# A four-layer graph network on one core: the last layer as seven block products merged by TensorE, gate values kept in PSUM, and a plan that models the shared port

## The chip, the cores and the metric

The kernel runs on one core of one Trainium2 chip. The metric is the device time of one execution in microseconds; the time of the kernel is the median of its runs. The engines are TensorE (PE; its weight loads are PEld), VectorE (DVE), ScalarE (ACT), GpSimd (POOL) and SyncE (SP), which issues nearly all DMA transfers. PSUM, into which TensorE writes, has eight banks of 512 float32 columns; the kernel calls them slots.

## The reference

x is 64 graphs of 256 nodes with 128 features; adj is one 256 x 256 adjacency matrix that all graphs share. Four layers follow each other, each with a residual and a layer norm. Two are attention layers. The third is a gated network of five steps. The fourth is a graph convolution with powers of adj. Cut to what matters:

```python
def _L2_gnn_ref(input, in_matrix, out_matrix, ...):
    def step(h, _):
        m_in = jnp.einsum('nm,bmd->bnd', in_matrix, h)
        m_out = jnp.einsum('nm,bmd->bnd', out_matrix, h)
        av = jnp.concatenate([m_in, m_out], axis=-1)
        u3 = h @ u3_w.T + u3_b
        z = jax.nn.sigmoid(av @ w3_w.T + w3_b + u3)
        r = jax.nn.sigmoid(av @ w4_w.T + w4_b + u3)
        hv = jnp.tanh(av @ w5_w.T + w5_b + (r * h @ u5_w.T + u5_b))
        h = (1.0 - z) * h + z * hv
        return (h, None)
    h, _ = jax.lax.scan(step, input, None, length=5)
    return h

def _L3_gnn_ref(x_1, adj0, adj1, weight_1):
    # _chebyshev(adj, x, 3): adj @ x, adj^2 @ x, adj^3 @ x, stacked
    parts = [x_1[..., None], _chebyshev(adj0, x_1, 3), _chebyshev(adj1, x_1, 3)]
    x_all = jnp.concatenate(parts, axis=3)
    return jnp.einsum('bnik,iok->bno', x_all, weight_1)

x = _layernorm(x + _L0_gnn_ref(x, adj, ...), axis=-1)
x = _layernorm(x + _L1_gnn_ref(x, adj, ...), axis=-1)
x = _layernorm(x + _L2_gnn_ref(x, adj, adj, ..., 5), axis=-1)
x = _layernorm(x + _L3_gnn_ref(x, adj, adj, L3_gnn_weight_1), axis=-1)
```

Since adj0 and adj1 are the same matrix, the last layer is x W0 + A x W1 + A² (x W2 + A x W3) with four combined weights, W0 holding the identity of the residual too.

## The kernel before

The 64 graphs go through in 32 units of two graphs. A unit's tile has 128 partitions and four blocks of 128 columns (two graphs, two halves of the nodes). Ten units are in flight, each in its own lane of SBUF buffers; a lane takes its next unit when it has finished one. All arithmetic is float32.

**The order.** No loop fixes what runs next. `spawn` writes a unit's operations down as tasks, each with its engine, a duration in ns, and what it reads and writes. `Plan.run` then plays a clock: each engine takes, among the tasks whose inputs are there and whose PSUM slots are free, the one with the smallest key, and is busy for the duration given; the result is visible to others after LATENCY. The key (`first`) is the unit's number times PERIOD, plus the task's due time (durations and latencies along its dependences, times PACE or, in the third layer, PACE_GATED), less HASTE for a task on a slot already open. The outcome is one fixed list for each engine, and the chip runs these lists in order with semaphores between them. So a wrong duration in the plan costs nothing by itself, but an instruction that waits on the chip holds all that stands behind it on its engine, of every unit.

**The left product** (`left_fast`, L833 to L878, matmuls all at L844) computes adj times a tile by seven 128-column products in place of eight. GpSimd forms three sums of blocks (`block_sums`, L833, L835, L836), TensorE makes seven products into two slots, ScalarE copies two of them out (L856, L859), VectorE merges (L865, L875, L877, L878). The second product accumulates on the first in its slot after L856 has copied the first out.

**The gated step** (`layer2`) makes five 512-column products (`product`, all at L902): three into slot ps_g (for r, then z added on it) and two into ps_v. ScalarE takes tanh of r (L914), of z (L922) and of the candidate v (L931) into SBUF tiles, which the profile calls e and p. VectorE does four 512-wide operations: (r+1) h (L917), (z-1) h (L929), (z+1) v (L933), and the sum (L935). Then a block transpose (L943 or L956) and DMA transfers through DRAM bring the state into the other layout. ps_g is free again when L922 has read it.

**The last layer** (`layer3`) makes one left product, then, for units 0 to 28, eight 256-column products with the four weights (L1004), two copies by ScalarE (L1009, L1010), block sums by VectorE, seven 128-column products with blocks of the squared adjacency (in `one`, L1015), a copy (L1028) and five merges by VectorE. The last PLAIN = 3 units use `layer3_end`: eight 256-column products with the weights (L1051), two copies (L1055), four 256-column products with the squared adjacency (L1058). A layer norm and the transfer to the output follow.

Of the kernel before, what the change touches and what calls it, by code (L numbers as in the profile page):

```python
# [13 lines left out]
P = 128  # L14
# [18 lines left out]
PERIOD = 46000.0  # L33
TAIL = 0.3
LATE = 6
PACE = 3.0
PACE_GATED = 1.65
# [4 lines left out]
HASTE = {"pe": 10000.0, "act": 10000.0, "dve": 10000.0}  # L42
PLAIN = 3
# [4 lines left out]
class Cell:  # L48


    def __init__(self, ap=None, bank=False, over=()):
        self.ap, self.bank = ap, bank

        self.over = list(over)
        for c in over:
            c.over.append(self)
        self.writers, self.readers, self.users = [], [], 0
        self.group, self.waits = None, set()


class Task:
    def __init__(self, eng, ns, fn, unit, wait, dma):
        self.eng, self.ns, self.fn, self.unit, self.wait, self.dma = eng, ns, fn, unit, wait, dma
        self.step, self.layer = 0, 0
        self.deps, self.then, self.left, self.at = set(), [], 0, 0.0
        self.off = self.end = self.due = 0.0
        self.banks, self.takes = [], []


class Plan:  # L70
# [5 lines left out]
    LATENCY = {"pe": 500, "dve": 400, "act": 400, "pool": 500, "sp": 3500}  # L76
# [4 lines left out]
    def __init__(self, banks):  # L81
        self.free_banks = list(banks)
        self.tasks = []
        self.unit, self.step, self.layer = -1, 0, 0

        self.rank = None

    def add(self, eng, ns, fn, reads=(), writes=(), after=(), wait=0, group=None, dma=False):
        t = Task(eng, ns, fn, self.unit, wait, dma or eng == "sp")
# [27 lines left out]

    def run(self, spawn, units, key):
# [4 lines left out]
        free = dict.fromkeys(ready, 0.0)  # L123
        seen, now, running = 0, 0.0, []
# [16 lines left out]
        def start(lane):  # L141
            mine = [u for u in queue if u % LANES == lane]
            if mine:
# [5 lines left out]
                for t in self.tasks[seen:]:  # L149
                    t.due = max([d.due + (PACE_GATED if t.layer == 2 else PACE) * (d.ns + (  # L150
                        d.wait + self.LATENCY["sp" if d.dma else d.eng] if d.dma or d.eng != t.eng else self.OWN[t.eng]))
                        for d in t.deps if d.unit == t.unit], default=0.0)
                enlist()
# [4 lines left out]
        while any(ready.values()) or running:  # L158

            for t in [t for t in running if t.end <= now]:  # L160
                running.remove(t)
                for c in t.banks:
                    c.users -= 1
                    if not c.users:
                        self.free_banks.append(c.ap)
# [3 lines left out]
            for e, tasks in ready.items():  # L169
# [3 lines left out]
                fit = [t for t in tasks if t.at <= now + (HOLD if now < START else 0) and len(t.takes) <= len(self.free_banks)]  # L173
                if not fit:
                    continue
                t = min(fit, key=key)
# [3 lines left out]
                for c in t.takes:  # L180
                    c.ap = self.free_banks.pop(0)
                order.append(t)
                free[e] = t.off = now + t.ns
# [20 lines left out]
def kernel(  # L204
# [51 lines left out]
    def bank():  # L256
        return Cell(bank=True)
# [5 lines left out]
    def lane_cells(k):  # L263
# [8 lines left out]
        for at, halves in (("e", (("r", "ex"), ("z",))), ("p", (("v",), ("xT1",)))):  # L272
            for half, names in enumerate(halves):
                over = [c[at]]
                for name in names:
                    c[name] = Cell(c[at].ap.rearrange("p g n -> p (g n)")[:, half * T : (half + 1) * T], over=over)
                    over = [*over, c[name]]
        c["x"] = cell(f"x_{k}", [P, UB, NC, D])
# [213 lines left out]
    w3 = cell("w3", [D, 2, 2, D])  # L492
    add(POOL, 480, lambda: nc.gpsimd.tensor_add(w3.ap[:, 0, 1, :], wk.ap[:, :, 0], ident.ap), (wk, ident), (w3,))
    for k in range(1, 4):
        add(POOL, 480, lambda k=k: nc.gpsimd.tensor_add(
            w3.ap[:, k % 2, 1 - k // 2, :], wk.ap[:, :, k], wk.ap[:, :, k + 3]), (wk,), (w3,))
# [10 lines left out]
    fast_blocks(a2f, a2T)  # L507
    plan.rank = None


    X = {}

# [7 lines left out]
    def small(u, what, ns, op, reads, writes, **more):  # L520

        pool = u >= TIGHT and what in SMALL
        add(POOL if pool else DVE, 300 if pool else ns, lambda: op(nc.gpsimd if pool else nc.vector), reads, writes, **more)
# [56 lines left out]
    def layernorm(u, L, pairs, swap=False, centred=False):  # L580
# [11 lines left out]
        add(POOL, 1150, lambda: nc.gpsimd.tensor_tensor(rstd.ap, ve.ap, nhalf.ap, op=ALU.pow), (ve, nhalf), (rstd,))  # L592
        by_act = u >= TIGHT and plan.layer in NORM

        if by_act and not centred:
            mean = st.ap.rearrange("p k (j s) -> p k j s", j=2)[:, :, :, 1]
            if "shift" in SMALL:
                add(POOL, 330, lambda: nc.gpsimd.tensor_scalar_mul(
                    nm.ap.rearrange("p (k j) -> p k j", k=2), mean, -1.0), (st,), (nm,))
                add(POOL, 250, lambda: nc.gpsimd.tensor_mul(ve.ap, nm.ap, rstd.ap), (nm, rstd), (ve,))  # L600
# [48 lines left out]
    def layer0(u, L):  # L649
# [47 lines left out]
        for b in range(UB):  # L697
            add(DVE, 540, lambda b=b: nc.vector.tensor_add(
                ev[:, b, :, 0:P].rearrange("p k (c i) -> p k c i", c=NC), rv()[:, b].rearrange("p c (i k) -> p k c i", k=2),
                neg0.ap[:, :, 0:P].rearrange("p k (c i) -> p k c i", c=NC)), (row, neg0), (e,), group=es)  # L700
# [23 lines left out]
        if not SCALES or u < TIGHT:  # L724
            add(DVE, 700, lambda: nc.vector.tensor_mul(
                h.ap[:, :, 0 : D + 2], h.ap[:, :, 0 : D + 2],
                rs.ap.rearrange("p (g o) -> p g o", o=1).to_broadcast([P, G, D + 2])), (h, rs), (h,))
# [28 lines left out]
    def layer1(u, L):  # L756
# [6 lines left out]
        for bs in [[b] for b in range(UB)] if u < HALVES else [list(range(UB))]:  # L763
# [3 lines left out]
            for b in bs:  # L767
# [7 lines left out]
                mask1.ap.rearrange("p (o c) n -> p o (c n)", o=1).to_broadcast([P, n, NC * N])), (ec, mask1), (pc,))  # L775
# [36 lines left out]
        add(DVE, 600, lambda: nc.vector.scalar_tensor_tensor(hp.ap, ex.ap, 1.0, hp.ap, op0=ALU.min, op1=ALU.max), (ex, hp), (hp,))  # L812
        add(DVE, 630, lambda: nc.vector.tensor_add(hp.ap, hp.ap, xf), (hp, X[u]), (hp,))
# [11 lines left out]
    def block_sums(src, blk, s, by_pool):  # L825
# [5 lines left out]
        wide, narrow = (780, 580) if by_pool else (350, 215)  # L831

        add(by, wide, lambda: eng.tensor_sub(  # L833
            four[:, 0:2], blk(slice(2, 3)).to_broadcast([P, 2, D]), blk(slice(0, 4, 3))), (src,), (s,), group=ss)
        add(by, narrow, lambda: eng.tensor_sub(four[:, 2:3], four[:, 1:2], blk(slice(0, 1))), (src, s), (s,), group=ss)  # L835
        add(by, narrow, lambda: eng.tensor_add(four[:, 3:4], four[:, 2:3], blk(slice(1, 2))), (src, s), (s,), group=ss)  # L836
        return four

    def left_fast(src, blk, mat, s, p1, m, by_pool):
# [26 lines left out]
        merged(y, m, ms)  # L866

# [12 lines left out]
    def layer2(u, L):  # L880
        h, ht = turned(u, L, -1), X[u]
        for step in range(STEPS):
# [3 lines left out]
            if fast and not step:  # L886
                left_fast(ht, lambda g, ht=ht: ht.ap.rearrange("p b c d -> p (b c) d")[:, g], adjf, L["r"], L["z"], m, step in BY_POOL)
            elif fast:
                left_fast(ht, lambda g, ht=ht: gd(ht.ap)[:, g], adjTf, L["r"], L["z"], m, step in BY_POOL)
# [9 lines left out]
            ps_g, ps_v = bank(), bank()  # L899

            def product(ps, w, c, rhs, start, stop, after=()):
# [5 lines left out]
            merge = plan.tasks[at:][-4:]  # L907
            product(ps_g, lambda: gT.ap[:, 3], gT, h, True, False, merge[2:3] if fast else lefts[1:2])
# [5 lines left out]
            add(ACT, 590, lambda ps_g=ps_g, up=up: nc.scalar.activation(  # L914
                r.ap, ps_g.ap, AF.Tanh, bias=bias2.ap[:, 1:2], scale=0.5 / up), (ps_g, bias2), (r,))
            tanh_r = list(r.writers)
            add(DVE, 650, lambda h=h: nc.vector.scalar_tensor_tensor(r.ap, r.ap, 1.0, h.ap, op0=ALU.add, op1=ALU.mult),  # L917
                (r, h), (r,))
            product(ps_v, lambda: gT.ap[:, 2], gT, m, True, False, tanh_r)
            product(ps_g, lambda: gT.ap[:, 0], gT, m, False, True)  # L920
            product(ps_v, lambda: u5T.ap[:, 0], u5T, r, False, True)
            add(ACT, 590, lambda ps_g=ps_g, up=up: nc.scalar.activation(  # L922
                z.ap, ps_g.ap, AF.Tanh, bias=bias2.ap[:, 0:1], scale=0.5 / up), (ps_g, bias2), (z,))

            new = L["xT1" if h is L["xT0"] else "xT0"]
            if not step:
                add(ACT, 600, lambda h=h, new=new, part=part: nc.scalar.mul(new.ap, h.ap, part), (h,), (new,))
                h = new
            add(DVE, 650, lambda h=h, new=new: nc.vector.scalar_tensor_tensor(  # L929
                new.ap, z.ap, -1.0, h.ap, op0=ALU.add, op1=ALU.mult), (z, h), (new,))  # L930
            add(ACT, 590, lambda ps_v=ps_v, up=up: nc.scalar.activation(  # L931
                v.ap, ps_v.ap, AF.Tanh, bias=bias2.ap[:, 2:3], scale=1 / up), (ps_v, bias2), (v,))
            add(DVE, 650, lambda: nc.vector.scalar_tensor_tensor(v.ap, z.ap, 1.0, v.ap, op0=ALU.add, op1=ALU.mult),  # L933
                (v, z), (v,))
            add(DVE, 650, lambda new=new, part=part: nc.vector.scalar_tensor_tensor(  # L935
                new.ap, v.ap, part, new.ap, op0=ALU.mult, op1=ALU.subtract), (v, new), (new,))
# [36 lines left out]
        if far(u, STEPS - 1):  # L973
            add(DVE, 600, lambda: nc.vector.tensor_add(
                y.ap.rearrange("p (g a i) -> p g a i", g=G, i=BL), ht.ap.rearrange("p (a g i) -> p g a i", g=G, i=BL),
                X[u].ap.rearrange("p b c (a i) -> p (b c) a i", i=BL)), (ht, X[u]), (y,))
# [6 lines left out]
    def layer3(u, L):  # L983
        xT = turned(u, L, STEPS)
        aT, s = L["m"], L["z"]
        if STEPS in FAST and far(u, STEPS):
            left_fast(X[u], lambda g: X[u].ap.rearrange("p b c d -> p (b c) d")[:, g], adjf, L["r"], L["z"], aT, STEPS in BY_POOL)
            tail = [t for t in plan.tasks[-4:-3]]
# [11 lines left out]
        x, y = bank(), bank()  # L1000
        home = {(0, 0): (x, slice(0, 2)), (1, 1): (x, slice(2, 4)), (0, 1): (y, slice(0, 3, 2)), (1, 0): (y, slice(1, 4, 2))}
        for k, src in enumerate((xT, aT)):
            for (b, c), (ps, at) in home.items():
                add(PE, mm_ns(N), lambda k=k, src=src, c=c, b=b, ps=ps, at=at: nc.tensor.matmul(  # L1004
                    gd(ps.ap)[:, at], bn(src.ap)[:, b, c * P : (c + 1) * P], w3.ap[:, k],
                    start=(k == 0 and b == 0), stop=(k == 1), skip_group_check=True), (src, w3), (ps,), tail)
        four, sv = gd(L["xT1"].ap), gd(s.ap)
        copies = object()
        add(ACT, 270, lambda: nc.scalar.copy(sv[:, 0:4:3], gd(x.ap)[:, 0:3:2]), (x,), (s,), group=copies)  # L1009
        add(ACT, 270, lambda: nc.scalar.copy(sv[:, 1:3], gd(y.ap)[:, 0:2]), (y,), (s,), group=copies)  # L1010
        block_sums(s, lambda g: sv[:, g], L["xT1"], -1 in BY_POOL)
        t, p1, out = L["xT1"], L["v"], L["ht"]

        def one(ps, at, lhs, c, k, start, after=()):
            return add(PE, mm_ns(P) + 4, lambda: nc.tensor.matmul(  # L1015
                ps.ap[:, at * P : (at + 1) * P], a2f.ap[:, k // NC, k % NC * P : (k % NC + 1) * P], lhs(), start=start,
                stop=True, skip_group_check=True), (c, a2f), (ps,), after, group=four)

        def d(g):
            return lambda: sv[:, g]  # L1020

        def sm(k):
# [95 lines left out]
```

The softmax here doesn't subtract the row's maximum and nothing guards it: scores larger than these inputs give would overflow.

## Time and profile before

| | before |
|---|---|
| median of 3 runs | 1388.74 us (1388.68 to 1389.56) |
| the profiled run: time, span of the profile | 1389.4 us, 1387.4 us |
| instructions in the profile | 23,294 |
| granted TensorE clock | 1.00 |
| HBM traffic | 81.10 MB read, 64.46 MB written, 105 GB/s |

The span runs from the first to the last instruction of the profile. Busy times are those of one execution; a float32 product of the program stands in the trace as two matmul records. An operation is named by its line, its engine and its tiles (written <- read), where `ps` is any of the eight slots. The chain of waits follows the work that ended last back to the start. Idle time of an engine that does not bound the kernel costs nothing.

### The profile page before, as it was taken

The numbers are of one execution on the slowest core, as the hardware profiler recorded it, in microseconds if no ns is written. First come the engines' busy times: TensorE is split into PE (matmuls) and PEld (weight loads), VectorE is DVE, ScalarE is ACT, GpSimd is POOL, SyncE is SP. The second block draws the span as 40 slices with busy tenths as digits, with TensorE's granted clock in tenths as the row PEclk, the third lists the DMA queues.
The fourth block names the chain that finished last, engine by engine and source line by source line (L and its number), as shares of the span: only waits on it lengthen the run. The fifth ranks groups of instructions, "written<-read, shape, count | busy, mean of one in ns | idle before, by whom it ended". The sixth has DMA issues, their size and how long they took to land.

```text
span 1387.4 us, 23294 instructions
## 1 busy us (share of the span) xinstructions
PE 1379.3 (99%) x6891; PEld 966.9 (70%) x6891; DVE 1195.8 (86%) x2745; ACT 943.7 (68%) x2303; POOL 629.9 (45%) x1039
## 2 busy tenths in 40 slices
PE   9999999999999999999999999999999999999998
PEld 9776666766676766676766777777666666667777
DVE  6978999998888898888988798899888888998865
ACT  5887656666766777766677678887766655565544
POOL 4234343534355454455354454465443533536433
PEclk9999999999999999999999999999999999999999
DMA  4224545454555555554545554545454454554322
GB/s 129 38 47 103 113 106 106 109 128 111 113 121 107 108 123 105 120 115 104 119 109 115 116 119 115 110 110 121 107 128 100 104 108 95 112 124 115 82 65 61
DMA packets 530077, 147.13 MB, mean 106 GB/s; under 512 B 456480, under 2 KB 495136, under 8 KB 529952
## 3 DMA queue, kind: packets, MB, share of 16 engines
q1 hardware_dynamic: 529152, 145.13, 47.0%
q8 instruction: 55, 0.90, 0.3%
q14 instruction: 70, 0.57, 0.2%
q10 hardware_dynamic: 800, 0.52, 0.1%
HBM read 81.10 MB, written 64.46 MB: 105 GB/s over the span
## 4 chain that ended last, share of the span: by engine, by line
PE 91%; DVE 6%; ACT 1%; issue 1%; POOL 1%; DMA 0%; SPq 0%; POOLq 0%; DVEq 0%; ACTq 0%
PE ps L902 45%; PE ps L844 19%; PE ps L1004 7%; PE ps L743 4%; PE ps L780 4%; PE ps L1015 3%; PE ps L738 2%; PE ps L667 2%; PE ps L792 2%; PE ps L821 1%; PE ps L1051 1%; DVE p L933 1%; DVE st L587 1%; DVE p L546 0%; DVE e L917 0%
## 5 line engine op out<-in xcount | busy, mean ns | idle before, releaser
L902 PE MATMUL ps<-m,gT 128*128 128x512 f32 x960 | 478.6, 593 | 0.0
L902 PEld LDWEIGHTS ps<-m,gT 128*128 128x128 f32 x960 | 166.1, 191 | 113.0 <-issue 91.5
L833 POOL TENSOR_TENSOR e<-ht 128x256 f32<-128x256 f32 x121 | 104.3, 862 | 210.1 <-DMA ht<-hb 153.5
L844 PEld LDWEIGHTS ps<-adjTp,ht 128*128 128x128 f32 x726 | 124.0, 191 | 82.7 <-issue 73.3
L914 ACT ACTIVATE e<-ps,bias 128x512 f32<-128x512 f32 x160 | 109.9, 687 | 95.0 <-PE ps L902 88.4
L931 ACT ACTIVATE p<-ps,bias 128x512 f32<-128x512 f32 x160 | 109.7, 686 | 85.2 <-PE ps L902 83.9
L902 PE MATMUL ps<-e,u5T 128*128 128x512 f32 x320 | 163.2, 593 | 0.0
L592 POOL TENSOR_TENSOR rstd<-ve,nhalf 128x4 f32<-128x4 f32 x126 | 143.6, 1141 | 34.8 <-DVE ve L589 29.8
L589 POOL TENSOR_SCALAR ve<-st 128x4 f32<-128x4 f32 x110 | 38.4, 349 | 259.3 <-DVE st L587 231.3
L844 PE MATMUL ps<-adjTp,e 128*128 128x128 f32 x968 | 149.6, 275 | 0.0
L922 ACT ACTIVATE e<-ps,bias 128x512 f32<-128x512 f32 x160 | 109.8, 688 | 55.5 <-PE ps L902 55.2
L844 PEld LDWEIGHTS ps<-adjTp,e 128*128 128x128 f32 x968 | 130.5, 192 | 13.8 <-issue 11.1
L844 PE MATMUL ps<-adjTp,ht 128*128 128x128 f32 x726 | 138.9, 275 | 0.3 <-DMA ht<-hb 0.2
L933 DVE SCALAR_TENSOR_TENSOR p<-e,p 128x512 f32<-128x512 f32 x160 | 115.2, 721 | 19.4 <-ACT p L931 19.1
L902 PEld LDWEIGHTS ps<-e,u5T 128*128 128x128 f32 x320 | 58.9, 190 | 63.8 <-issue 49.0
L611 ACT ACTIVATE x<-ht,ve,rstd 128x128 f32<-128x128 f32 x212 | 92.4, 489 | 14.3 <-POOL ve L600 14.2
L902 PE MATMUL ps<-xT,gT 128*128 128x512 f32 x192 | 98.0, 593 | 0.0
L875 DVE TENSOR_TENSOR m<-ps,m 128x256 f32<-128x256 f32 x182 | 75.0, 412 | 18.5 <-PE ps L844 17.3
L833 POOL TENSOR_TENSOR e<-x 128x256 f32<-128x256 f32 x61 | 48.7, 798 | 91.8 <-ACT x L611 78.5
L769 ACT ACTIVATE e<-m,esd 128x256 f32<-128x256 f32 x116 | 84.3, 767 | 0.5 <-DMA m<-row 0.5
L917 DVE SCALAR_TENSOR_TENSOR e<-e,xT 128x512 f32<-128x512 f32 x96 | 68.6, 715 | 16.4 <-ACT e L914 15.6
L844 PEld LDWEIGHTS ps<-adjT,x 128*128 128x128 f32 x366 | 60.7, 191 | 29.2 <-issue 24.8
(211 smaller groups left out, 3201.9 us busy)
## 6 DMA issues: line engine op xcount, KB each, us to landing
hb<-p SPq DMA_DIRECT2D x182, 256.0 KB, 2.3
ht<-hb SPq DMA_DIRECT2D x484, 64.0 KB, 2.5
xT<-hb SPq DMA_DIRECT2D x244, 64.0 KB, 2.5
m<-row SPq DMA_DIRECT2D x58, 256.0 KB, 3.7
hb<-p SPq DMA_DIRECT2D x124, 64.0 KB, 1.8
ht<-hb SPq DMA_DIRECT2D x31, 256.0 KB, 2.8
out_dram<-x SPq DMA_DIRECT2D x30, 256.0 KB, 2.5
m<-in_x_dram SPq DMA_DIRECT2D x88, 64.0 KB, 2.4
```

The costliest lines, as they stand in the source:

```text
L592: add(POOL, 1150, lambda: nc.gpsimd.tensor_tensor(rstd.ap, ve.ap, nhalf.ap, op=ALU.pow), (ve, nhalf), (rstd,))
L611: add(ACT, 400, lambda j=j, b=b, ch=ch, view=view, at=at, shift=shift, col=col: nc.scalar.activation(X[u].ap[:, b, ch, :], view()[:, j, :] ...
L769: add(ACT, 660 if u >= DIRECT_ROWS else 360, lambda g=g, b=b: nc.scalar.activation(e.ap[:, g, :].rearrange("p (c n) -> p c n", c=NC), ev() ...
L833: add(by, wide, lambda: eng.tensor_sub(four[:, 0:2], blk(slice(2, 3)).to_broadcast([P, 2, D]), blk(slice(0, 4, 3))), (src,), (s,), group=ss)
L844: add(PE, mm_ns(P) + 4, lambda: nc.tensor.matmul(ps.ap[:, at * P : (at + 1) * P], lhs(), mat.ap[:, k, c * P : (c + 1) * P], start=start, s ...
L875: add(DVE, 335, lambda: nc.vector.tensor_tensor(mv[:, 1:3], pv(y)[:, 0:2], mv[:, 3:4].to_broadcast([P, 2, P]), op=ALU.add), (y, m), (m,))
L902: add(PE, mm_ns(T), lambda: nc.tensor.matmul(ps.ap, w(), rhs.ap, start=start, stop=stop, skip_group_check=True), (c, rhs), (ps,), after)
L914: add(ACT, 590, lambda ps_g=ps_g, up=up: nc.scalar.activation(r.ap, ps_g.ap, AF.Tanh, bias=bias2.ap[:, 1:2], scale=0.5 / up), (ps_g, bias2 ...
L922: add(ACT, 590, lambda ps_g=ps_g, up=up: nc.scalar.activation(z.ap, ps_g.ap, AF.Tanh, bias=bias2.ap[:, 0:1], scale=0.5 / up), (ps_g, bias2 ...
L931: add(ACT, 590, lambda ps_v=ps_v, up=up: nc.scalar.activation(v.ap, ps_v.ap, AF.Tanh, bias=bias2.ap[:, 2:3], scale=1 / up), (ps_v, bias2), ...
L933: add(DVE, 650, lambda: nc.vector.scalar_tensor_tensor(v.ap, z.ap, 1.0, v.ap, op0=ALU.add, op1=ALU.mult), (v, z), (v,))
L1004: add(PE, mm_ns(N), lambda k=k, src=src, c=c, b=b, ps=ps, at=at: nc.tensor.matmul(gd(ps.ap)[:, at], bn(src.ap)[:, b, c * P : (c + 1) * P], ...
```

## The change

1. **The last layer of units 0 to 27** goes from `layer3` to a new `layer3_blocks`. The weight is treated as the squared adjacency was: a 2 x 2 block matrix, in seven products in place of eight. Each of the seven multiplies two 128-row halves, so it is a pair of 128-column matmuls; the four sums of inputs are made by GpSimd on 256 columns. Merging moves to TensorE: ScalarE copies a product that several results share from slot x to slot y ("seeds" it), and later products accumulate on that seed or on what lies in x already. A seeded slot has to be one all of whose columns a matmul has written before, which `Cell.full`, `seeded_bank`, `fits` and `take` keep track of.
2. **PLAIN** goes from 3 to 4: unit 28 takes the form of the last units. The two halves of w3 change places, and `fast_blocks(w3f, w3)` makes four more weight blocks in the setup.
3. **Gates**: tanh of z is written back to ps_g, and VectorE writes z times v there; tanh of r and of v stay in SBUF. The z product of m is listed ahead of the first v product.
4. **The plan**: VectorE operations with two SBUF inputs and all GpSimd operations are marked `port`. A marked one starts after the other engine's marked one has let go, and after a marked VectorE task another one gets TURN = 12000 added to its key. Several durations and latencies change. HASTE applies to a task between two uses of a slot (`hold`, `within`), and VectorE gets none. PERIOD, LATE, PACE and PACE_GATED change.

```diff
-PERIOD = 46000.0
+PERIOD = 41000.0
-LATE = 6
-PACE = 3.0
-PACE_GATED = 1.65
+LATE = 5
+PACE = 4.0
+PACE_GATED = 1.56
-HASTE = {"pe": 10000.0, "act": 10000.0, "dve": 10000.0}
-PLAIN = 3
+HASTE = {"pe": 45000.0, "act": 45000.0}
+IN_PSUM = (0, 1, 0, 1)
+TURN = 12000.0
+PLAIN = 4
...
-    LATENCY = {"pe": 500, "dve": 400, "act": 400, "pool": 500, "sp": 3500}
+    LATENCY = {"pe": 400, "dve": 350, "act": 350, "pool": 900, "sp": 4000}
...
-                t = min(fit, key=key)
+                t = min(fit, key=lambda t: key(t) + (TURN if twice and t.port and e == "dve" else 0))
...
-                free[e] = t.off = now + t.ns
+                begin = now
+                if t.port:
+                    begin = max(now, held["pool" if e == "dve" else "dve"])
+                free[e] = t.off = begin + t.ns
...
-            ps_g, ps_v = bank(), bank()
+            ps_g, ps_v = bank(True), bank(True)
...
+            product(ps_g, lambda: gT.ap[:, 0], gT, m, False, True)
             product(ps_v, lambda: gT.ap[:, 2], gT, m, True, False, tanh_r)
-            product(ps_g, lambda: gT.ap[:, 0], gT, m, False, True)
...
+            tz, tv = ps_g if IN_PSUM[1] else z, ps_v if IN_PSUM[2] else v
+            add(ACT, 590, lambda ps_g=ps_g, up=up, tz=tz: nc.scalar.activation(
+                tz.ap, ps_g.ap, AF.Tanh, bias=bias2.ap[:, 0:1], scale=0.5 / up), (ps_g, bias2), (tz,))
...
+            vv = (v, ps_g, ps_v)[IN_PSUM[3]]
+            add(DVE, 600, lambda tz=tz, tv=tv, vv=vv: nc.vector.scalar_tensor_tensor(
+                vv.ap, tz.ap, 1.0, tv.ap, op0=ALU.add, op1=ALU.mult), (tv, tz), (vv,), port=not (IN_PSUM[1] or IN_PSUM[2]))
+            add(DVE, 600, lambda new=new, part=part, vv=vv: nc.vector.scalar_tensor_tensor(
+                new.ap, vv.ap, part, new.ap, op0=ALU.mult, op1=ALU.subtract), (vv, new), (new,), port=not IN_PSUM[3])
...
+        layer3_blocks(u, L, xT, aT, tail)
...
+        x, y = bank(), seeded_bank()
+        pair(x, 0, x0, xT, 0, tail, True, (y,))
+        first = copied(lambda y=y: part(y, 0, 2), x, 0, 2, y, group)
+        pair(x, 0, sums[2], sb_, 5, [*first, *late])
+        second = copied(lambda y=y: part(y, 2, 2), x, 0, 2, y, group)
+        pair(x, 2, sums[1], sa, 4)
+        copied(lambda: gd2(p1.ap), x, 2, 2, p1, None)
+        pair(y, 0, a0, aT, 2, first)
+        copied(lambda: D4[:, 0:2], y, 0, 2, direct, ds)
+        pair(x, 0, sums[0], sa, 6, second)
+        held = added(gd2(up.ap), 2, x, 0, gd2(p1.ap), (p1,), up, None)
+        pair(y, 2, sums[3], sb_, 3, second)
+        added(E[:, 0:2], 2, y, 2, gd2(p1.ap), (p1,), mv, es)
+        pair(x, 0, a1, aT, 7, held)
+        copied(lambda: D4[:, 2:4], x, 0, 2, direct, ds)
...
+        x, y, os_ = bank(), seeded_bank(), object()
+        square(x, 0, 0, mv, E[:, 0], (), True, (y,))
+        first = copied(lambda: part(y, 0), x, 0, 1, y, group)
+        square(x, 0, 5, four, f[:, 2], first)
+        second = copied(lambda: part(y, 1), x, 0, 1, y, group)
+        square(x, 1, 4, four, f[:, 1])
...
+        square(y, 0, 2, mv, E[:, 1], first)
...
+        square(x, 0, 6, four, f[:, 0], second)
...
+        square(y, 1, 3, four, f[:, 3], second)
...
+        square(x, 0, 7, up, E[:, 5], held)
```

`pair` is two 128-column matmuls, `square` one, `copied` a copy by ScalarE, `added` an addition by VectorE.

## The prediction

> **What bounds the kernel now.** I read four views in this order: busy times, the slices, the chain of waits, and the timeline of TensorE's matmuls. The first three, from the page:
>
> ```profile
> PE 1379.3 (99%) x6891; PEld 966.9 (70%) x6891; DVE 1195.8 (86%) x2745; ACT 943.7 (68%) x2303; POOL 629.9 (45%) x1039
> ...
> PE   9999999999999999999999999999999999999998
> ...
> DVE  6978999998888898888988798899888888998865
> ...
> PEclk9999999999999999999999999999999999999999
> ...
> PE 91%; DVE 6%; ACT 1%; issue 1%; POOL 1%; DMA 0%; SPq 0%; POOLq 0%; DVEq 0%; ACTq 0%
> ```
>
> TensorE is busy in every slice at full clock, and 91% of the chain that ends last is matmuls. But a matmul's end is modelled, so "busy 99%" may hide gaps. What does not lie is the distance between starts, which the timeline of TensorE gives:
>
> ```profile
> 701.15 1.02 PE L902 MATMUL ps<-m,gT 128*128 128x512 f32 x2
> 702.01 0.38 PE L844 MATMUL ps<-adjTp,ht 128*128 128x128 f32 x2
> 702.23 0.39 PE L844 MATMUL ps<-adjT,x 128*128 128x128 f32 x2
> ...
> 706.56 0.83 PE L844 MATMUL ps<-adjTp,e 128*128 128x128 f32 x6
> 707.23 0.39 PE L844 MATMUL ps<-adjT,x 128*128 128x128 f32 x2
> ```
>
> A program's product is two records. A 512-column product takes 702.01 - 701.15 = 0.86 us, a 128-column one 0.22 us: (707.23 - 706.56) / 6 = 0.112 us a record. Over all 6891 records the median distance is 429 ns for 512 columns (1600 records), 216 ns for 256 (900), 112 ns for 128 (3081). Summing what each distance has over its width's median leaves 13.0 us: 4.2 in the first 40 us, 5.8 behind the last matmul, and only 3.0 in the 1340 us between. So TensorE is not merely busy but streaming almost without a gap. A product taken away is worth its distance, and other engines matter only through gaps they cause.
>
> How the last stage reads, from the timeline of the end:
>
> ```profile
> 1356.22 1.06 PE L1015 MATMUL ps<-p,a2T 128*128 128x128 f32 x8
> 1356.42 0.27 ACT L1028 COPY p<-ps 128x128 f32<-128x128 f32 x1
> 1356.47 0.69 DVE L933 SCALAR_TENSOR_TENSOR p<-e,p 128x512 f32<-128x512 f32 x1
> ...
> 1359.92 0.69 DVE L978 TENSOR_TENSOR m<-ps,x 128x512 f32<-128x512 f32 x1
> ...
> 1369.75 1.89 PE L1051 MATMUL ps<-w,xT 128*128 128x256 f32 x8
> ...
> 1371.48 1.89 PE L1051 MATMUL ps<-w,m 128*128 128x256 f32 x8
> ...
> 1379.68 2.19 PE L1058 MATMUL ps<-e,a2T 128*128 128x256 f32 x8
> ```
>
> (1371.48 - 1369.75) / 8 = 0.216 us again. A 512-wide VectorE operation with one input in PSUM (L978) takes 0.69 us, as one with both in SBUF does (L933).
>
> **What the Trainium skill says.** "TensorE: Matmul & The Clock Gate", section on the 56 ns gap: warm matmuls start N / 2.4 GHz plus some 2.5 ns apart, 55.6 ns at N = 128 and 215.7 at 512. The trace agrees at twice these (112 and 429): a float32 record streams its columns twice. So a narrow product pays its fixed cost more often: 2 x 112 = 224 against 216 ns. "SBUF — State Buffer", section Who interferes with whom: a VectorE instruction with two SBUF inputs and a GpSimd one that reads SBUF exclude each other for a whole instruction; with one SBUF input VectorE does not contend. The trace agrees: L875, which reads PSUM, has median 0.414 and 95th percentile 0.425 us; L933, with two SBUF inputs, 0.68 and 1.01; GpSimd's L836 0.46 and 0.94. "PSUM — Partial Sum Buffer", The four PSUM rules: writes by ScalarE or VectorE do not change the bits that decide whether a matmul adds or overwrites, which is what the seeded slots rely on; no row of before shows such a seed.
>
> **The change, part by part.**
>
> *The last layer's products (28 of 32 units).* Before, units 0 to 28 ran 8 products of 256 columns (L1004, 464 records = 29 x 16) and 7 of 128 (L1015, 406 = 29 x 14): 16 x 216 + 14 x 112 = 5024 ns a unit. Units 29 to 31 ran the plain form, 12 products of 256 (24 records): 5184 ns. After, units 0 to 27 run seven pairs for the weight and seven single products for the squared adjacency, 21 of 128 columns: 42 x 112 = 4704 ns; units 28 to 31 run plain. Before: 29 x 5.024 + 3 x 5.184 = 161.2 us. After: 28 x 4.704 + 4 x 5.184 = 152.4 us. **-8.8 us of TensorE**, all on the path.
>
> *Its merges.* VectorE lost three block sums (455, 384, 319 ns) and five merges (413, 413, 283, 414, 278): 2.96 us a unit; it gets three 256-wide adds and four 128-wide ones, 3 x 413 + 4 x 280 = 2.36. In all 29 x 2.96 - 28 x 2.36 = 20 us off. ScalarE goes from two copies of 256 (371) and one of 128 (265), 1.0 us, to five and two, 2.39: 28 x 2.39 - 29 x 1.0 = +38 us, busy 944 to about 982. GpSimd gains five 256-wide (about 0.84) and two 128-wide (0.6) instructions, 5.4 us a unit, 151 us: 630 to 781, 57% of the span. None is the bound, so I price them at nothing: the matmuls of the nine other units in flight lie over them. What they can cost is a TensorE wait: a product on top of a seed waits for the copy that wrote it, some 0.37 us plus the 0.16 us of a matmul's drain (275 - 112 ns), and behind it stand the whole queue's matmuls of all units. Seven such steps a unit. If the order leaves others between, 0; if half of each shows, 7 x 0.27 x 28 = 53 us. The nearest row for how well the order hides this is the left product: its second product waits in the same way for the copy L856, 182 times, and TensorE's gaps of the whole middle are 3.0 us, under 0.02 us each. I take 0; by that row 28 x 7 x 0.02 = 4 us is the upper end.
>
> *z's tanh and z times v in PSUM.* Three of the four VectorE gate operations lose one SBUF input: L929, L933, L935, 160 each, 115.1 + 115.2 + 116.8 = 347 us busy. At 0.685 without contention 480 of them take 329: 18 us off VectorE, which comes to about 1158 us, 84%. ScalarE's and VectorE's writes to PSUM have no row. The PSUM page's table of engine access calls ScalarE faster to PSUM than to SBUF; I allow 0.1 us of their 0.69 either way, 16 us of ScalarE's time in all and as much of VectorE's, off the path while both stay under 90%. The cost is in slots: z's slot was free when tanh z ended and is now held until L935 ends. Over the 160 steps those ends lie 6.03 us apart on average, beside the 6.18 us from the slot's first matmul to the end of tanh z. 160 x 6.03 = 965 us of slot time, of 8 x 1387 = 11,099: 9% more. My sum of what is held now (gate slots 160 x (6.2 + 6.6), left products 182 x (3.6 + 8.0), last layer 29 x 2 x 14, layers 0 and 1 an estimate: seven slots a unit at 5 us, between the 3.6 and 8.0 of the left product) is about 6100, 55%; then some 65%. I take 0 for it; bound below.
>
> *Order and costs in the plan.* The plan's durations, latencies, priorities and the port change the order of one static queue for each engine, not the work. Its latency is 400 ns behind a matmul and 350 behind VectorE and ScalarE. The timeline has a tanh starting 1.06 us after its 512-column product starts, where the plan now allows 1.26; and VectorE 0.72 us after a tanh starts, where it allows 0.94. So it still errs to the safe side. The most it can win is the 3.0 us of middle gaps and a part of the 4.2 and 5.8 at the ends, which I bound at 2 us; it can lose through them as much.
>
> *Free edits.* Five more GpSimd instructions in the setup (blocks of the weight), hidden: the first last layer starts at 168.6 us, and GpSimd is busy 11 of the 40 us from 20 to 60. The swapped halves of w3, the tile names over old buffers and the slot choice move nothing on the chip. SP's queue issues the same transfers in all 32 units; none is moved past another by design.
>
> Sum: -8.8 + 0 + 0 + 0. The span of the profile, 1387.4, comes to 1378.6; the runs lie 1.3 us over it (median 1388.74; the profiled run itself 1389.4), so **1379.9 us**.
>
> **Rivals.** (a) *More than the products*: middle gaps and part of the ends go too, -8.8 - 3 to -5: about 1375.5. For it: less contention, longer latencies allowed behind GpSimd (900 ns) and DMA (4000). Against: only 3 us are there. (b) *Eaten*: the seven dependent steps of the last layer show as waits of some 0.3 us a unit for the seed (28 x 0.3 = 8.4): about 1388, no change. For it: seven round trips TensorE to ScalarE instead of one. Against: 182 left products do that already without a gap. (c) *Slots run out, slower*: with z's slot held twice as long, all eight are at times held by units that wait for VectorE; TensorE then has nothing to open. It decides from 8.8 / 160 = 0.055 us a step on; at 0.12 us a step, 19 us, the time is 1399. For it: the hold doubles in the layer that takes most of the span, and VectorE, which frees the slot, is the second busiest engine. Against: about a third of the slots is free on average, and VectorE's load falls. The change doing something else than it says I see no room for: the products can be counted.
>
> **How the numbers follow.** Forecast 0.60 (1377.5 to 1385, holding the 4 us bound), (a) 0.20, (b) 0.10, (c) 0.10. A difference of 0.2%, 2.8 us, is about what measurement can tell from none: faster is the forecast and (a), 0.80; within, (b), 0.10; slower, (c), 0.10. The range runs from 1374.5 (all middle gaps and 2 us at the ends gone) to 1387: outside are (c), most of (b) and a little below.
>
> **What would show it.** 28 x 28 = 784 records of the weight's pairs and 392 of the square, 7221 records in all, with 112 ns between starts; gaps in the middle of about 3 us again; VectorE near 1158, ScalarE near 982, GpSimd below 781; L929, L933 and L935's successors near 0.685 us with little spread. Wrong if the sum of gaps grows by over 6 us: at seed copies it is (b), at first matmuls of a gate slot (c).

## The result, and the profile after

The changed kernel takes 1382.05 us, median of 4 runs (1382.03 to 1382.75), where the kernel before takes 1389.15 (1388.68 to 1389.72) beside it. The ratio is 0.995, with a 95% interval of 0.9933 to 0.9967: 7.1 us faster, where 8.8 were forecast and 1379.9 us in all. On another chip (run 5) the ratio was 0.9948 (0.9933 to 0.9963).

The busy times, slices and chain of the page after:

```profile
PE 1371.9 (99%) x7221; PEld 970.5 (70%) x7221; DVE 1167.7 (85%) x2709; ACT 972.2 (70%) x2414; POOL 691.3 (50%) x1240
...
PE   9999999999999999999999999999999999999998
...
PEclk9999999999999999999999999999999999999999
...
PE 98%; DVE 1%; ACT 0%; issue 0%; POOL 0%; POOLq 0%; DVEq 0%; ACTq 0%
```

TensorE bounds the kernel as before, now with 98% of the chain. There are 330 records more (7221), although less is streamed: narrow products are counted as often as wide ones. The timeline of TensorE alone shows their pace:

```profile
701.75 0.61 PE L1088 MATMUL ps<-w,xT 128*128 128x128 f32 x4
702.20 0.61 PE L1088 MATMUL ps<-w,p 128*128 128x128 f32 x4
702.65 0.39 PE L904 MATMUL ps<-adjT,x 128*128 128x128 f32 x2
...
704.23 0.46 PE L904 MATMUL ps<-adjTp,e 128*128 128x128 f32 x2
704.52 0.39 PE L904 MATMUL ps<-adjT,e 128*128 128x128 f32 x2
```

L1088 is now every product of the last layer's block form, L904 the left products, L963 the gate products. (702.20 - 701.75) / 4 = 0.112 us a record, the pace of any 128-column product. Between 704.23 and 704.52 lie 0.29 us for two records that need 0.22: a gap of some 70 ns, and such gaps are what the rest of this text counts.

The account is the prediction's: each record at its width's distance (429, 216, 112 ns) is the streamed time; what the distances have over it is gap, up to 40 us, in the middle, and behind the last matmul. From the two traces, in us:

| | span | streamed | before the first | gaps to 40 us | gaps in the middle | behind the last |
|---|---|---|---|---|---|---|
| before | 1387.43 | 1373.06 | 1.35 | 4.23 | 3.07 | 5.73 |
| after | 1380.23 | 1364.26 | 1.34 | 3.03 | 5.86 | 5.75 |
| difference | -7.20 | **-8.80** | 0 | -1.20 | **+2.79** | 0 |

The stream fell by exactly the 8.8 us forecast; 1.6 us of it went back into gaps. (The time is 2.1 us above the forecast; the other 0.5 us is the distance of the time from the span, 1.8 us in the run profiled here where 1.3 were assumed.) On the face of it the case is closed. The runs show that it isn't: the two halves of the change are worth much more, with opposite signs, than the sum tells.

### The profile page after: what moved, and what is told of

It is laid out like the page before. It is cut to its first block, busy times and chain, and to the rows that moved or that the text cites. A ratio compares the mean times of both kernels' runs of the same rounds, so it can differ in the third digit from the quotient of the medians.

```text
span 1380.2 us, 24466 instructions
## 1 busy us (share of the span) xinstructions
PE 1371.9 (99%) x7221; PEld 970.5 (70%) x7221; DVE 1167.7 (85%) x2709; ACT 972.2 (70%) x2414; POOL 691.3 (50%) x1240
## 4 chain that ended last, share of the span: by engine, by line
PE 98%; DVE 1%; ACT 0%; issue 0%; POOL 0%; POOLq 0%; DVEq 0%; ACTq 0%
PE ps L963 50%; PE ps L904 20%; PE ps L1088 10%; PE ps L840 4%; PE ps L803 4%; PE ps L727 2%; PE ps L852 2%; PE ps L798 2%; PE ps L881 1%; PE ps L1157 1%; PE ps L1164 0%; PE ps L405 0%; PE ps L593 0%; PE ps L1031 0%; PE ps L636 0%; PE ps L752 0%
## 5 line engine op out<-in xcount | busy, mean ns | idle before, releaser
L963 PE MATMUL ps<-m,gT 128*128 128x512 f32 x960 | 473.3, 593 | 0.0
L963 PEld LDWEIGHTS ps<-m,gT 128*128 128x128 f32 x960 | 168.0, 191 | 131.8 <-issue 114.4
L975 ACT ACTIVATE e<-ps,bias 128x512 f32<-128x512 f32 x160 | 109.8, 687 | 94.7 <-PE ps L963 85.8
L649 POOL TENSOR_SCALAR ve<-st 128x4 f32<-128x4 f32 x110 | 26.8, 244 | 278.4 <-DVE st L647 269.6
L963 PE MATMUL ps<-e,u5T 128*128 128x512 f32 x320 | 163.5, 592 | 0.0
L904 PEld LDWEIGHTS ps<-adjTp,ht 128*128 128x128 f32 x726 | 118.6, 191 | 61.2 <-issue 48.6
L652 POOL TENSOR_TENSOR rstd<-ve,nhalf 128x4 f32<-128x4 f32 x126 | 137.5, 1091 | 47.5 <-DVE ve L649 41.4
L904 PE MATMUL ps<-adjTp,e 128*128 128x128 f32 x968 | 149.0, 276 | 0.2 <-ACT m L919 0.2
L984 ACT ACTIVATE ps<-ps,bias 128x512 f32<-128x512 f32 x160 | 105.6, 661 | 55.1 <-PE ps L963 54.3
L893 POOL TENSOR_TENSOR e<-ht 128x256 f32<-128x256 f32 x121 | 96.9, 801 | 88.1 <-DMA ht<-hb 73.1
L904 PEld LDWEIGHTS ps<-adjTp,e 128*128 128x128 f32 x968 | 129.6, 192 | 11.9 <-issue 7.9
L996 DVE SCALAR_TENSOR_TENSOR ps<-ps,p 128x512 f32<-128x512 f32 x160 | 110.2, 689 | 32.0 <-ACT p L993 31.4
L904 PE MATMUL ps<-adjTp,ht 128*128 128x128 f32 x726 | 136.7, 275 | 0.0
L963 PEld LDWEIGHTS ps<-e,u5T 128*128 128x128 f32 x320 | 58.7, 190 | 63.1 <-issue 55.5
L963 PE MATMUL ps<-xT,gT 128*128 128x512 f32 x192 | 98.2, 593 | 0.0
L978 DVE SCALAR_TENSOR_TENSOR e<-e,xT 128x512 f32<-128x512 f32 x96 | 72.2, 752 | 12.9 <-ACT e L975 12.4
L919 ACT COPY m<-ps 128x128 f32<-128x128 f32 x182 | 48.0, 268 | 44.0 <-PE ps L904 35.0
```

What stands on the lines that cost most here:

```text
L652: add(POOL, 1010, lambda: nc.gpsimd.tensor_tensor(rstd.ap, ve.ap, nhalf.ap, op=ALU.pow), (ve, nhalf), (rstd,))
L893: add(by, wide, lambda: eng.tensor_sub(four[:, 0:2], blk(slice(2, 3)).to_broadcast([P, 2, D]), blk(slice(0, 4, 3))), (src,), (s,), group=s ...
L904: add(PE, mm_ns(P) + 4, lambda: nc.tensor.matmul(ps.ap[:, at * P : (at + 1) * P], lhs(), mat.ap[:, k, c * P : (c + 1) * P], start=start, s ...
L963: add(PE, mm_ns(T), lambda: nc.tensor.matmul(ps.ap, w(), rhs.ap, start=start, stop=stop, skip_group_check=True), (c, rhs), (ps,), after)
L975: add(ACT, 590, lambda ps_g=ps_g, up=up, tr=tr: nc.scalar.activation(tr.ap, ps_g.ap, AF.Tanh, bias=bias2.ap[:, 1:2], scale=0.5 / up), (ps_ ...
L984: add(ACT, 590, lambda ps_g=ps_g, up=up, tz=tz: nc.scalar.activation(tz.ap, ps_g.ap, AF.Tanh, bias=bias2.ap[:, 0:1], scale=0.5 / up), (ps_ ...
```

## Experiments

Each run stands beside the kernel before on the same chip. Three chips served, and those medians are 1391.09 us on the first (runs 1 to 4), 1390.23 on the second (runs 5 to 8) and 1389.87 on the third (runs 9 to 12). Ratios carry 95% intervals. Gaps are from the trace of one execution of each run. What two traces of the same kernel differ by is seen in run 5: 6.6 us in the middle against 5.9.

**1. The last layer of before in the changed kernel.**

```diff
-PLAIN = 4
+PLAIN = 3
-        layer3_blocks(u, L, xT, aT, tail)
+        x, y = bank(), bank()
+        ...   (the form of before, its weight layout, its layer3_end)
```

> The changed kernel with the last layer, the weight layout and PLAIN = 3 of before put back; gates in PSUM, port model and all constants of the plan stay. Theory A (the time is TensorE's stream plus gaps; the gain is the products): the streamed time is that of before again, 1373.1 us, so 1388 to 1391 us, the whole gain lost. Theory B (the gain comes from the port model and the gates in PSUM, the last layer's saving being eaten by its round trips): 1381 to 1384 us.

Measured: 1388.07 us, ratio 0.9977 (0.9967 to 0.9986). Streamed 1373.06, gaps 2.79 to 40 us, 2.74 in the middle. The stream is back, and the time lies within theory A's range. Not all of the gain goes with it: gates and plan alone are worth 0.2%. In this run GpSimd is busy 551.2 us where it was 629.9 before, so gates and plan take contention away here too, and the gaps in the middle hardly show it (2.7 against 3.1).

**2. The new last layer alone on the kernel before.**

```diff
-IN_PSUM = (0, 1, 0, 1)
+IN_PSUM = (0, 0, 0, 0)
-        t.port = port or eng == "pool"
+        t.port = False
...   (PERIOD, LATE, PACE, PACE_GATED, HASTE, LATENCY, the durations and the order of the z and v products as before)
```

> The kernel before with the new last layer and PLAIN = 4 alone: gates in SBUF, no port in the plan, durations, latencies, priorities and constants of before. Theory A: streamed 1364.3 us, so 1379 to 1384 us, the gain whole or nearly. Theory B: 1387 us or more, since the round trips of the last layer show without the better plan.

Measured: 1400.55 us, ratio 1.0068 (1.0056 to 1.008): slower than before by 9.5 us. The streamed time is 1364.26, as theory A said, but the gaps in the middle are 22.4 us (6.4 of them behind 1355 us, where the work runs out; before has 0.3 there). Theory A fails, and my prediction's "0" for the last layer's merges with it; theory B's range holds.

**3. The changed kernel with its gates in SBUF.**

```diff
-IN_PSUM = (0, 1, 0, 1)
+IN_PSUM = (0, 0, 0, 0)
```

> The changed kernel with tanh of z and z times v in SBUF again (and so marked as users of the port in the plan). Streamed time unchanged, 1364.3 us. Theory A: 1380 to 1384 us, only the gaps may differ by 2 us either way. Theory B: the contention is back, 1385 us or more. Theory C (the longer hold of z's slot made the 2.8 us of added gaps in the middle): 1379 to 1380 us.

Measured: 1397.97 us, ratio 1.005 (1.0036 to 1.0063). Gaps in the middle 22.1 us, about as many as in run 2 without the new plan (22.4, though 6.4 of those lie at the end and only 0.5 here). So the new plan alone does not mend the new last layer. Whether the two tiles in PSUM do, or the order that changed with them, run 9 tells. Theory B's range holds. Theory C, that the longer hold of z's slot made the added gaps, is out. The busy times of this run against those of after show where to look:

```profile
PE 1378.7 (99%) x7221; PEld 970.7 (70%) x7221; DVE 1203.8 (86%) x2709; ACT 974.1 (70%) x2414; POOL 782.6 (56%) x1240
```

The same 1240 GpSimd instructions take 782.6 us instead of 691.3. One place in its timeline (start, duration, engine and line) holds the longest gap:

```profile
253.47 1.21 DVE L833 TENSOR_TENSOR p<-e,mask 128x1024 f32<-128x1024 f32 x1
253.48 2.98 POOL L1080 TENSOR_TENSOR p<-xT,m 128x256 f32<-128x256 f32 x1
...
254.60 0.68 DVE L991 SCALAR_TENSOR_TENSOR xT<-e,p 128x512 f32<-128x512 f32 x1
...
255.20 0.68 DVE L996 SCALAR_TENSOR_TENSOR p<-e,p 128x512 f32<-128x512 f32 x1
...
255.92 1.10 DVE L998 SCALAR_TENSOR_TENSOR xT<-p,xT 128x512 f32<-128x512 f32 x1
...
256.52 0.49 PE L1088 MATMUL ps<-w,p 128*128 128x128 f32 x2 [2.73 <-POOL p L1080]
```

L1080 is one of the four sums of inputs; undisturbed it takes 0.73 us, here 2.98. It was issued at 253.48, 10 ns behind L833; its end at 256.46 less 0.73 is 255.73, some 0.15 us from the end of L996 at 255.88. So it looks as if three VectorE operations, each with two SBUF inputs, went ahead of it, and then L998 took 1.10 us instead of 0.68, as if it had waited in its turn. The profile doesn't show the port itself; this is read from the overlap in time. TensorE stood for 2.73 us. That agrees with what the Trainium skill says in "SBUF — State Buffer", Who interferes with whom: the pair of ports that VectorE and GpSimd share is held for a whole instruction and the other side blocks.

**4. Less to stream, nothing else.** Two of the eight 256-column products of the last layer are left out of the kernel before.

```diff
             for (b, c), (ps, at) in home.items():
+                if k and b == c:
+                    continue
                 add(PE, mm_ns(N), ...
```

> The kernel before without two of the eight 256-column products of the last layer in units 0 to 28 (two of the four that add the adjacency's half; the output leaves these terms out), nothing else changed. Theory A: 29 x 4 records x 216 ns = 25.1 us less, so 1364 us, to within 3 us. Theory B (another engine stands right behind TensorE, VectorE with 86%): at most half of that, 1376 us or more.

Measured: 1368.11 us, ratio 0.9835 (0.9821 to 0.9848), 23 us under before. Streamed 1348.00, that is 25.06 less; gaps in the middle 6.8. Stream turns into time almost one for one, and no other engine becomes the bound within these 25 us. This confirms the bound and refutes theory B of that run.

**5. The changed kernel again**, unchanged, on the second chip.

> The changed kernel as it is, beside the others of this call. All theories: 7 us under the kernel before of the same chip.

Measured: 1382.77 us, ratio 0.9948 (0.9933 to 0.9963); gaps in the middle 6.6.

**6. Is it the new sums on GpSimd?** Run 3 with the four L1080 left out of each unit; the tasks stay in the plan, so that every engine keeps its order.

```diff
-            add(POOL, 705, lambda k=k, i=i, op=op, j=j: nc.gpsimd.tensor_tensor(sums[k], i, j, op=op), cells, (cell_,), group=group)
+            add(POOL, 705, lambda: None, cells, (cell_,), group=group)
-        late = sb_.writers[-2:-1]
+        late = sb_.writers[-2:-1]; sums = [x1, x0, a1, a0]
```

> The changed kernel with its gates in SBUF and with the four 256-wide sums of inputs of the last layer (28 x 4 GpSimd instructions) left out, the pairs taking plain inputs instead, so that the output is another one; every engine's order is that of the run with the gates in SBUF. Theory D (GpSimd and VectorE shut each other out; with the last layer's sums on GpSimd and the gates in SBUF there is too much of both): the middle gaps fall from 22 us to 8 or less, 12 us or more under the run with the gates in SBUF, so 4 us or more under the kernel before. Theory E (what the gates in SBUF cost is the order of VectorE's and ScalarE's work or slots, not the shared port): gaps of 18 us or more stay, at least 3 us over before.

Measured: 1393.8 us, ratio 1.0027 (1.0017 to 1.0038). Gaps 17.0 us: 5.1 fewer than in run 3, GpSimd down to 680.6 us. It lies between the two theories' bounds, close to theory E's. The sums are a part of the loss, the 2.7 us wait above among it, but with GpSimd as little busy as after, 17 us stay. Theory D in the form "too much on GpSimd" falls; whether order or port makes the 17 us, run 9 tells.

**7. Half of the gates.** z in PSUM, z times v in SBUF: L996 and L998 change, L998 having two SBUF inputs again.

```diff
-IN_PSUM = (0, 1, 0, 1)
+IN_PSUM = (0, 1, 0, 0)
```

> The changed kernel with tanh of z in PSUM but z times v in SBUF: two of the three VectorE operations freed from the port are still free of it, and z's slot is let go one operation earlier. Theory D: gaps between 6 and 12 us, 1 to 6 us slower than the changed kernel. Theory C (the longer hold of z's slot costs time): as fast or faster than the changed kernel.

Measured: 1390.94 us, ratio 1.0007 (0.9999 to 1.0016), so 8 us slower than the changed kernel beside it; gaps 15.0. More than theory D's upper end. Letting z's slot go one operation earlier did not help, which speaks against slots a second time. But the order changed here too, and a redraw alone is worth 4.7 us of gaps (run 10), more than the 3 us by which theory D's range is exceeded.

**8. The plan without the port.**

```diff
-        t.port = port or eng == "pool"
+        t.port = False
```

> The changed kernel with the port left out of the plan (no task is marked, so no task is put off for the other engine and TURN never applies); the work is the same. Theory D with the port on the chip alone deciding: within 3 us of the changed kernel. Rival (the plan's model of the port is what keeps the gaps small): 5 us or more slower.

Measured: 1388.47 us, ratio 0.9987 (0.998 to 0.9994), 5.7 us slower than the changed kernel; gaps 12.3 in the middle. The rival's side: at the gates in PSUM the order is worth some 6 us. Whether that is the model's merit or the luck of one order, run 10 asks.

**9. The same order, gates in SBUF.** Runs 3 and 7 changed the plan's inputs, and so the order, with the tiles. Here the plan is that of the changed kernel and only the tiles in the emitted instructions differ.

```diff
-                tz.ap, ps_g.ap, AF.Tanh, bias=bias2.ap[:, 0:1], ...
+                z.ap, ps_g.ap, AF.Tanh, bias=bias2.ap[:, 0:1], ...
-                vv.ap, tz.ap, 1.0, tv.ap, op0=ALU.add, op1=ALU.mult), ...
+                v.ap, z.ap, 1.0, v.ap, op0=ALU.add, op1=ALU.mult), ...
...   (L991 reads z, L998 reads v)
```

> The changed kernel's order on every engine, instruction for instruction, but tanh of z and z times v go to their SBUF tiles. Theory D (the shared port itself stalls TensorE): the gaps in the middle come to 15 us or more, as in the run whose plan knew of the SBUF tiles (22 us), 9 us or more slower than the changed kernel. Theory F (most of those 22 us came from another order, drawn because the plan's inputs changed): 7 to 12 us of gaps, 1 to 6 us slower than the changed kernel.

Measured: 1398.73 us, ratio 1.0063 (1.0048 to 1.0078); gaps in the middle 23.5 us, against 5.9 in the same order with the tiles in PSUM. Theory F falls, theory D's forecast holds: 17.6 us are the tiles' place and not the order. The busy times of this run:

```profile
PE 1380.6 (99%) x7221; PEld 971.1 (69%) x7221; DVE 1215.7 (87%) x2709; ACT 972.2 (70%) x2414; POOL 796.2 (57%) x1240
```

The groups of GpSimd and VectorE (busy us, mean ns of one, then idle before):

```profile
L996 DVE SCALAR_TENSOR_TENSOR p<-e,p 128x512 f32<-128x512 f32 x160 | 121.5, 760 | 26.8 <-ACT p L993 26.3
...
L998 DVE SCALAR_TENSOR_TENSOR p<-p 128x512 f32<-128x512 f32 x96 | 76.3, 795 | 1.0
L895 POOL TENSOR_TENSOR e<-e,ht 128x128 f32<-128x128 f32 x121 | 75.1, 621 | 6.0
```

and the same groups of the changed kernel:

```profile
L996 DVE SCALAR_TENSOR_TENSOR ps<-ps,p 128x512 f32<-128x512 f32 x160 | 110.2, 689 | 32.0 <-ACT p L993 31.4
...
L998 DVE SCALAR_TENSOR_TENSOR p<-ps,p 128x512 f32<-128x512 f32 x96 | 65.4, 682 | 1.0
...
L895 POOL TENSOR_TENSOR e<-e,ht 128x128 f32<-128x128 f32 x121 | 62.2, 515 | 6.0
```

With the same instructions in the same order GpSimd is busy 796.2 us against 691.3, VectorE 1215.7 against 1167.7. Both engines lose: L998 113 ns each, and L895, a sum of the left product that has nothing to do with the gates, 106 ns. One thing else differs: tanh of z takes ScalarE 687 ns into SBUF against 661 into PSUM, and no run tells whether a part of the 17.6 us comes from that. It can't be what lengthens L895. What TensorE's weight loads then waited for (us in all, times, longest):

```profile
PEld ps L963 <- DVE m L939: 7.6, 21, 0.9
PEld ps L904 <- ACT e L916: 6.4, 15, 1.1
PEld ps L963 <- DVE e L978: 4.7, 14, 0.8
...
PEld ps L904 <- POOL e L893: 4.2, 4, 2.1
```

The waits are spread over short dependences of many units, merges (L939) and copies (L916) first; GpSimd itself is only one of the releasers. A weight load can wait without TensorE standing still, so the gaps themselves count more. Each put down to the product that starts late, in us:

| gaps ahead of | changed kernel | run 9 |
|---|---|---|
| left products (L904) | 1.7 | 12.3 |
| gate products (L963) | 1.6 | 5.7 |
| the new last layer's products (L1088) | 1.5 | 3.6 |
| all others | 1.1 | 1.9 |

So the loss does not stand mainly where the edit was made. Most of it is ahead of the left products, whose inputs GpSimd sums. A late VectorE or GpSimd delays whatever stands behind it in its queue.

**10 and 11. Another order, the same work.**

```diff
-PERIOD = 41000.0
+PERIOD = 41500.0
```

> The changed kernel with PERIOD 41500 in place of 41000: the same work, the same tiles, another order. Theory F (the order is drawn anew by any change of the plan's inputs, and most draws are worse than the two kernels'): gaps of 9 to 20 us in the middle, 3 to 14 us slower than the changed kernel. Theory D: within 2 us of the changed kernel.

Measured: 1386.57 us, ratio 0.9975 (0.9965 to 0.9984); gaps 10.5 us, 4.7 more than after.

```diff
-PERIOD = 46000.0
+PERIOD = 46500.0
```

> The kernel before with PERIOD 46500 in place of 46000: the same work, another order. Theory F: gaps of 6 to 20 us in the middle (3.1 before), 3 to 16 us slower than before. Theory D: within 2 us of before.

Measured: 1390.57 us, ratio 1.0005 (0.9997 to 1.0014); gaps 4.4 us, 1.4 more. An order drawn by a change of 1% in one constant costs the changed kernel some 4 us (ratio 0.9975 against 0.995 and 0.9948), and the kernel before less than can be measured. For the changed kernel that is theory F at its lower end; for the kernel before it is theory D. With one redraw of each, this gives no spread, but run 8's 6 us can't be told from such a draw.

**12. The fourth gate operation too.**

```diff
-IN_PSUM = (0, 1, 0, 1)
+IN_PSUM = (1, 1, 0, 1)
```

> The changed kernel with tanh of r in PSUM too (in v's slot, which then waits for one VectorE operation): no gate operation of VectorE uses the port any more. Theory D: gaps of 6 us or less, as fast as the changed kernel or up to 3 us faster. Theory F: wherever the draw of its order puts it, 5 to 20 us of gaps, although VectorE and GpSimd are busy less. Theory C (holding slots longer costs): 10 us of gaps or more, with first matmuls of v's slot among them.

Measured: 1393.61 us, ratio 1.0022 (1.0015 to 1.0029). GpSimd is down to 659.8 us and VectorE to 1160.1, the least of all runs with the new last layer, and yet the gaps are 17.9 us, within theories F and C and far from D. Its waits say a part of why:

```profile
PEld ps L963 <- DVE e L978: 9.9, 29, 2.1
PEld ps L904 <- ACT e L916: 4.3, 15, 0.5
```

tanh of r now lies in v's slot, so the first product of v may start only when L978 has read it. Of the waits whose releaser the profile names, this one is the largest, with 29 cases, all of them at products that read m, as the first of v does; in the changed kernel L978 held all gate products' weight loads for 1.7 us. So theory C's sign is there, for v's slot. But only 3.4 of the 12 us of added gaps stand at these places. The others are ahead of left products (4.9) and of the last layer's (5.2), and the order was drawn anew; no run separates that. Less contention, but one more dependence between VectorE and TensorE, did not pay here.

No run that does the whole work beat the changed kernel.

## Why the prediction was right, and where it was right by luck

All gaps in the middle, from the traces, in us:

| last layer | gates | order | gaps in the middle |
|---|---|---|---|
| before | SBUF | before | 3.1 (4.4 redrawn) |
| before | PSUM | new plan (run 1) | 2.7 |
| new | SBUF | plan of before (run 2) | 22.4 |
| new | SBUF | new plan (run 3) | 22.1 |
| new | SBUF | that of the changed kernel (run 9) | 23.5 |
| new | PSUM | the changed kernel | 5.9, 6.6 (10.5 redrawn) |

- **The last layer's products, -8.8 us:** right to the digit, and run 4 shows that stream turns into time.
- **Its merges, priced at nothing** because "none is the bound": this step failed. With the gates in SBUF the new last layer costs 19 us of gaps (22.4 less 3.1), which is more than it saves; alone it makes the kernel slower by 9.5 us. Shares of 70% or 56% busy do not say that a delay is hidden when TensorE has only 1% of slack and every engine runs a fixed list. That idle time of an engine off the bound costs nothing, as said ahead of the prediction, does not carry over to its delays.
- **The gates, priced at nothing:** this failed too, the other way. They are worth 17.6 us in the order of the changed kernel (run 9); in the other two orders on record with the same tiles in PSUM (runs 8 and 10) the gaps are 12.3 and 10.5, so 10 to 12 us below the 22.1 of run 3. And they are worth it only beside the new last layer; with the old one the gaps hardly move (3.1 to 2.7). I had counted the 18 us of VectorE's contention and dropped them because VectorE was off the path. The forecast of the time came right because these two unpriced terms, +19 and -18, nearly cancel, and that is luck; that the order drawn for the changed kernel was the best of three is a part of it.
- **The seeds:** 0 taken, 4 us as upper end. The changed kernel has 12 gaps of over 40 ns ahead of L1088, 2.05 us together, where L1004 and L1015 had none. The timeline of after at one of them:

```profile
1260.87 0.36 ACT L1099 COPY ps<-ps 128x256 f32<-128x256 f32 x1 [0.42 <-PE ps L1088]
...
1261.28 0.30 PEld L1088 LDWEIGHTS ps<-w,p 128*128 128x128 f32 x2 [0.41 <-ACT ps L1099]
1261.28 0.49 PE L1088 MATMUL ps<-w,p 128*128 128x128 f32 x2 [0.22 <-ACT ps L1099]
```

  Here the product stands until the seed has been copied. But by the releasers that the profile names, only 0.7 of the 2.05 us stand behind copies from slot to slot, the short gaps right after them counted in; 0.4 stand behind a copy into SBUF and 0.9 behind VectorE's merge (L1135). So rival (b)'s mechanism is there at less than a tenth of its price, within the 4 us bound, and is at most a quarter of the 2.8 us by which the middle grew.
- **Slots, rival (c):** z's slot is held 12.28 us on average from first matmul to L998, against the 12.2 worked out, and this costs nothing visible: runs 3 and 7 let it go earlier and are slower, though contention and order changed with it. A slower kernel was a real possibility, but z's slot would not have been the reason. For v's slot run 12 does show such waits.
- **The plan, at most 5 us:** beside the old last layer it stays within this (run 1, plan and gates together: 1.4 us fewer gaps up to 40 us, 0.3 in the middle). Beside the new one a redraw costs 4.7 us of gaps and leaving the port out 6.4. The bound was drawn from the gaps that the kernel before had, and the new last layer can make more.
- **Loads:** VectorE 1167.7 (1158 forecast; L978 keeps two SBUF inputs, and its largest group went from 715 to 752 ns a piece, some 4 of the 10 us), ScalarE 972.2 (982), GpSimd 691.3 (below 781). Of these 90 us the new instructions are only 11: they take 140 us of the 151 forecast. The rest is GpSimd's other work, which got shorter as the gates left SBUF; with the old last layer (run 1) it is 79 us in all.

What stays open: why the kernel with the new last layer is so much more exposed. Its four sums on GpSimd explain 5.1 of some 16 us (run 6). Its own products show little of the loss, 3.3 of 22.4 us in run 2 and 3.6 of 23.5 in run 9 (7.0 of 22.1 in run 3), so waits inside its chain of round trips are not most of it. How the rest comes to products of other units, through its three further sums on GpSimd (L1121 to L1123), its added copies on ScalarE or the order, no run tells apart.

## What to carry to other kernels

When the bounding engine streams 99% of the time, take its work from start-to-start distances, and do not price work on the other engines at nothing because they are below 90%: ask which pairs of them share a port, and test the edit's halves apart. An edit that frees a shared resource can be worth nothing alone and decide whether its neighbour pays. Where a planner draws a static order, compare at least one redraw with the same work before reading a difference of 0.3% as an effect. And look for the gaps where they stand: they may fall on work that the edit did not touch.

## What the hardware showed that was not expected

A GpSimd sum of 0.73 us took 2.98 us while three VectorE operations with two SBUF inputs ran in a row (run 3); with the same order, GpSimd's whole work took 796.2 us instead of 691.3 when three gate operations of VectorE read SBUF alone (run 9). ScalarE's tanh of 512 columns took 661 ns into PSUM (L984) where before it took 688 into SBUF. VectorE's (z + 1) v of the same width took 689 ns on average with one input and the output in PSUM (L996), and 691 in the median from and to SBUF (run 9): writing PSUM cost it nothing that shows.
